# A decoder layer on one core: all expert slots add to the output directly, empty list entries add zero to foreign rows

## The chip, the cores and the metric

The kernel runs on 1 core of a Trainium2 chip. The metric is the device time of one execution in microseconds; the median of 3 runs of the kernel before is 553.12 (552.07 to 553.45). Five engines run beside each other: TensorE (PE, with PEld for its weight loads), VectorE (DVE), ScalarE (ACT), GpSimd (POOL) and SyncE (SP), which here only issues DMAs. Each works off its own instructions in program order and waits on semaphores for the others.

## The reference, cut to what matters

```python
x = x + attn(layernorm(x), ...)                 # 16 heads, latent keys = values
x = x + birwkv(layernorm(x), ctx, ctx, w, u)
# mixture of experts on h = layernorm(x): T = 2048 tokens, C = 256, F = 512, E = 8
logits = h @ router_w.T
weights, selected = sparsemixer_eval(logits, 0.01)       # two experts of each token
dense_w = zeros((T, E)); dense_w[tok, selected[:, n]] += weights[:, n]      # n = 0, 1
for e in range(E):
    out = out + dense_w[:, e:e+1] * ((silu(h @ w_gate[e].T) * (h @ w_up[e].T)) @ w_down[e].T)
return x + out
```

All is float32. Each token goes to 2 of 8 experts, so there are 4096 (token, expert) entries, and an expert's number of entries depends on the data.

## The kernel before, in words

**Order.** The program is written out by hand as steps s = 0, 1, ... (the loop at L1230). Each step has places "pre", "A", "B", "C", "D", and a plan (`at`, L1031) puts functions into them; each engine gets its instructions in that order. Steps 0 to 63 are the attention units (a unit is 4 heads of one of 16 sequences of 128 tokens; sequence b takes steps 4b to 4b+3). A unit's scores are made in step s, its maxima and exponentials follow, POOL divides them by their sums in step s+1 (`normalize`, L480), PE transposes them in step s+2 (`turn_probs`, L486) and multiplies by the values (L494). Between these, PE makes the queries of later sequences (L404) and the projections (`project`, L520), which need the last rows yP from a detour through DRAM (`rest_values`, L514, issued by SP).

**From a sequence to its entries.** About 8 to 12 steps after 4b, the second mixer's result is added to x (`mix_2`), the sum of both mixers is stored to the DRAM array acc (`store_sum`, L612), and its layernorm to the DRAM array xn2 (`store_row`, L631). Every 4 sequences make a route r (`route`, L666): DVE finds the two experts of 512 tokens, PE counts by prefix sums (L705 to L708) how many earlier tokens have chosen the same expert, and POOL scatters 16-byte entries (token, token, weight, 0) by indirect DMA to the DRAM array `lists` (L741), eight DMAs for a route, one a step. Expert e's entries stand in token order from row e x 2048. Before that, `blanks` (L278, step 5) has filled all of `lists` with empty entries: row to read 0, row to add to 2048 + a number below 128 (spare rows of acc), weight 0.

**Slots.** A slot is 128 consecutive entries of one expert. Which expert and which rows of `lists` a slot has is worked out on the chip in four tables (`table`, L773, on DVE): table 0 after 8 sequences has 9 slots that are full for sure, table 1 after 12 sequences 8 more, table 2 after all has 14 slots (whatever is left, partly filled ones among them), and table 3 has 8 full slots kept back for the end (`share`, L827, `last_table` L883, `very_last` L905). Table 2's three last slots (RARE) run only if the counts ask for them (`if_used`, L947); the other 36 (ORDER, L71) always run, one per step from step 64 on. The three conditional slots stand behind the 29th slot of the order (j = 28 at L1284), with seven to come. Table 2 is made in steps 75 to 77 by seven parts (L1180 to L1182), table 3 in steps 80 to 83.

**One slot.** `fetch` (L908, POOL) gathers 128 rows of xn2 three slots ahead. `bring` (L924) copies the expert's gate and up weights out of `wall` (all weights, resident in SBUF) by a register index, one on ACT, one on DVE (L934); every fourth slot ACT, DVE, PE load four register values. `turn` (L938) transposes the rows (L942) and copies them (xT, L944). `up` (L968) makes gate and up products (L980, 16 matmuls each), ACT takes silu (sl, L990) and DVE multiplies (hT, L992). `down` (L995) of the slot before makes the down products (L1002), DVE scales them by the entries' weights (y, L1013) and POOL adds the 128 rows by an accumulating indirect DMA (`add`, L1018). Each add waits until the one before has landed, as both may touch the same rows.

**Two targets.** Slots of tables 0 to 2 add to acc, which has 128 spare rows for the empty entries. At the first slot of table 3 a DMA copies acc's 2048 rows to the output (L1015), and the last eight slots, which are full, add to the output.

Of the kernel before, what the change touches and what calls it, by code (L numbers as in the profile page):

```python
# [18 lines left out]
P = 128  # L19
B = 16  # L20
# [34 lines left out]

# [7 lines left out]
S3 = 8  # L63
assert SF + S3 <= sure(B)
S2 = (2 * N + E * (P - 1)) // P - SF - S3
NS = SF + S2 + S3


SKIP = 3
# [10 lines left out]
def decoder_kernel(  # L80
# [38 lines left out]

    xn2 = dram.tile([N, C], F32, tag="xn2", name="xn2")  # L120
    lists = dram.tile([E * N + P, LW], I32, tag="lists", name="lists")
    acc = dram.tile([N + P, C], F32, tag="acc", name="acc")
# [84 lines left out]
    iotas = const.tile([P, max(*S1, S2, S3)], F32, tag="iotas", name="iotas")  # L207
# [8 lines left out]
    maskb = wpool.tile([P, HG, T], BF16, tag="maskb", name="maskb")  # L216
    QL = N // P
# [23 lines left out]
    def constants():  # L241
        for t, step, base in ((rev, -1, E), (eid, 1, 0), (ebase, N, 0)):
# [21 lines left out]
            pattern=[[1, max(*S1, S2, S3)]],  # L264
# [6 lines left out]

        nc.gpsimd.memset(blank, 0)
# [12 lines left out]
    wall = const.tile([P, E, WE], F32, tag="wall", name="wall")  # L285
# [325 lines left out]
    def store_sum(b):  # L611
        nc.sync.dma_start(acc[ts(b, T), :], xs[b])  # L612
# [53 lines left out]
    def route(r):  # L666
# [43 lines left out]
        )  # L710
        nc.vector.tensor_mul(d, d, kp)
# [26 lines left out]
        yield  # L738
        for k in range(RB):
            for n in range(2):  # L740
# [9 lines left out]
                nc.gpsimd.memset(pad, 0.0)  # L750
                yield
# [131 lines left out]
    def last_table():  # L883

        cnt = counts("2")
        full = whole(cnt, 0, "3")
        nc.vector.tensor_sub(full, full, took[0])
        yield
        last = share(full, S3, "3")
        both = rp.tile([P, E], F32, tag="both", name="both")  # L890
        nc.vector.tensor_add(both, took[0], last)
        took.append(last)
        yield
        left = whole(cnt, P - 1, "2")
        nc.vector.tensor_sub(left, left, both)
        yield from table(S2, left, both, "2")
# [7 lines left out]

    def very_last():  # L905
        return table(S3, took[1], took[0], "3")
# [61 lines left out]
    def up(j):  # L968
# [7 lines left out]
        def products():  # L976
            for o, w in zip((pg, pu), ws):
                for f in range(NF):
                    for c in range(NC):
                        nc.tensor.matmul(  # L980
                            o[:, ts(f, P)],
                            w[:, c * F + f * P : c * F + (f + 1) * P],
                            xT[:, c, :],
                            start=(c == 0),
                            stop=(c == NC - 1),
                        )

        products()
# [6 lines left out]
    def down(j):  # L995
# [18 lines left out]
        if j == SF + S2:  # L1014
            nc.sync.dma_start(out2, acc[0:N, :])  # L1015

        def add():
            nc.gpsimd.indirect_dma_start(  # L1018
                out=acc if j < SF + S2 else out2,
# [120 lines left out]
    for b in range(B):  # L1140
# [18 lines left out]
        if b % RB == RB - 1:  # L1159
# [70 lines left out]
    for s in range(SLOT0 + len(ORDER) + 1):  # L1230
# [111 lines left out]
```

## Time and profile before

| | us |
|---|---|
| median of 3 runs | 553.12 |
| the profiled execution's own time | 554.7 |
| its span in the profile | 553.0 |
| attention and routing (first matmul to the first slot's first product) | 6.5 to 321 |
| slots, some of them beside the last sequence's work | 321 to 538 |
| one slot, undisturbed | 5.52 |
| copy of acc issued by SP | 501.5 |
| last matmul ends | 537.9 |

How to read it: a page of the profile gives busy time, share and count of each engine, then the span in 40 slices with a digit for the busy share. A line of a timeline is: start, length, engine, line of the kernel, operation, written tile <- read tiles, size, count, and in brackets the idle time of that engine before it with what ended it. PEclk is the clock that TensorE was granted, as a share of full speed. A releaser is inferred; "issue" means that nothing visible was waited for.

The largest groups on PE are the slots' gate and up products (L980, 142.5 us with 1152 instructions), the projection (L520, 74.4), the scores (L442, 70.5), the down products (L1002, 68.0), the values (L494, 66.4) and the queries (L404, 65.3). On POOL they are the normalization (L480, 75.7 us, 64 times) and the adds to acc (L1018, 47.5 us, 28 times).

### The profile page before, as it was taken

How to read it: one execution, taken by the hardware profiler on the slowest of the kernel's cores; microseconds unless marked ns; L12 is line 12 of the kernel's file. 1: busy time of each engine (PE TensorE's matmuls, PEld its weight loads, DVE VectorE, ACT ScalarE, POOL GpSimd, SP SyncE). 2: the span in 40 equal slices, each digit the busy share in tenths (PEclk: the TensorE clock that was granted, in tenths of full speed). 3: DMA queues.
4: the chain of work that ended last, by engine and by line, in shares of the span. 5: the costliest groups of instructions: out<-in, count | busy, mean ns of one | idle time of the engine just before them, and what ended most of it. 6: DMA issues, size and time to landing. Idle time of an engine off the chain costs nothing. (4 is left out here: it accounts for less than half of the span.)

```text
span 553.0 us, 10138 instructions
## 1 busy us (share of the span) xinstructions
PE 512.8 (93%) x3272; PEld 439.2 (79%) x3272; DVE 330.6 (60%) x831; ACT 329.3 (60%) x953; POOL 327.1 (59%) x379
## 2 busy tenths in 40 slices
PE   4889999999999999999998989999989999989990
PEld 3768787887777887877875679989979999989980
DVE  3354776687887678888769776555644533333330
ACT  1788998898797888888986873434313232313200
POOL 5356647564787774697646976454875454541532
PEclk9999999999999999999998999999989999999996
DMA  5432245364365545131121113232234232325321
GB/s 149 98 88 67 70 133 170 121 198 120 110 182 133 170 130 178 41 98 37 52 79 56 40 53 66 38 65 45 40 40 51 48 51 47 51 47 173 58 30 19
DMA packets 39662, 47.59 MB, mean 86 GB/s; under 512 B 14136, under 2 KB 31416, under 8 KB 39576
## 3 DMA queue, kind: packets, MB, share of 16 engines
q1 hardware_dynamic: 30106, 37.20, 23.0%
q0 software_dynamic: 7936, 9.51, 11.2%
q8 instruction: 28, 0.46, 0.3%
q10 hardware_dynamic: 1566, 0.21, 0.3%
q14 instruction: 26, 0.21, 0.2%
HBM read 28.22 MB, written 13.31 MB: 75 GB/s over the span
## 5 line engine op out<-in xcount | busy, mean ns | idle before, releaser
L467 ACT ACTIVATE pr<-s,nm 128x128 f32<-128x128 f32 x256 | 90.7, 370 | 9.7 <-DVE nm L459 9.5
L480 POOL TENSOR_TENSOR pr<-pr,rsum 128x512 f32<-128x512 f32 x64 | 75.7, 1183 | 33.5 <-DVE rsum L479 25.6
L990 ACT ACTIVATE sl<-s 128x512 f32<-128x512 f32 x36 | 21.5, 598 | 120.7 <-PE s L980 104.9
L1018 POOL DMA_INDIRECT acc<-y,en x28 | 47.5, 1697 | 60.4 <-DVE y L1013 29.8
L442 PEld LDWEIGHTS s<-kvT,q 72*128 72x128 f32 x512 | 65.7, 191 | 18.7 <-issue 12.6
L980 PEld LDWEIGHTS s<-xT,w 128*128 128x128 f32 x576 | 70.5, 195 | 9.4 <-issue 6.7
L980 PE MATMUL s<-xT,w 128*128 128x128 f32 x576 | 72.0, 279 | 5.4 <-DVE xT L944 2.3
L520 PE MATMUL po<-outw_sb,yP 128*128 128x256 f32 x288 | 74.4, 385 | 0.6 <-DMA yP<-yd 0.6
L442 PE MATMUL s<-kvT,q 72*128 72x128 f32 x512 | 70.5, 279 | 3.2 <-DMA q<-qr 2.2
L980 PE MATMUL pu<-xT,w 128*128 128x128 f32 x576 | 70.5, 276 | 0.0
L992 DVE TENSOR_TENSOR hT<-sl,pu 128x512 f32<-128x512 f32 x36 | 24.7, 687 | 74.1 <-PE pu L980 56.9
L1002 PE MATMUL pd<-wall,hT 128*128 x288 | 68.0, 379 | 0.0
L494 PE MATMUL py<-aT,kvN 128*72 128x512 f32 x128 | 66.4, 600 | 1.6 <-ACT aT L488 1.3
L980 PEld LDWEIGHTS pu<-xT,w 128*128 128x128 f32 x576 | 67.7, 193 | 0.0
L404 PE MATMUL pq<-xnT,wq_sb 128*128 128x256 f32 x256 | 65.3, 387 | 0.0
L520 PEld LDWEIGHTS po<-outw_sb,yP 128*128 128x128 f32 x288 | 54.0, 193 | 13.1 <-issue 5.2
L459 DVE TENSOR_REDUCE nm<-s 128x4 f32<-128x512 f32 x64 | 43.6, 682 | 30.5 <-PE s L442 30.5
L1002 PEld LDWEIGHTS pd<-wall,hT 128*128 128x128 f32 x288 | 52.0, 190 | 5.6
L467 ACT ACTIVATION_READ_ACCUMULATOR pr<-s,nm 128x1 f32 x256 | 53.0, 207 | 0.0
L488 ACT COPY aT<-pt 128x512 f32<-128x512 f32 x64 | 37.2, 581 | 26.0 <-PE pt L486 24.6
L404 PEld LDWEIGHTS pq<-xnT,wq_sb 128*128 128x128 f32 x256 | 46.2, 195 | 5.0 <-issue 0.2
L912 POOL DMA_INDIRECT xr<-xn,en x36 | 37.4, 1040 | 13.3 <-issue 7.6
(172 smaller groups left out, 877.8 us busy)
## 6 DMA issues: line engine op xcount, KB each, us to landing
wall<-in_wg_dram SPq DMA_DIRECT2D x8, 512.0 KB
wall<-in_wu_dram SPq DMA_DIRECT2D x8, 512.0 KB
wall<-in_wd_dram SPq DMA_DIRECT2D x8, 512.0 KB
q<-q SPq DMA_DIRECT2D x16, 224.0 KB
yP<-yB SPq DMA_DIRECT2D x32, 112.0 KB
cx<-in_cx_dram SPq DMA_DIRECT2D x16, 128.0 KB
acc<-x SPq DMA_DIRECT2D x16, 128.0 KB
xn<-row SPq DMA_DIRECT2D x16, 128.0 KB
```

The source lines that it names most:

```text
L404: nc.tensor.matmul(pq[:, :GT], w[:, c, :], xnT[g][:, c, :], start=(c == 0), stop=(c == NC - 1))
L442: nc.tensor.matmul(ps[:, j, :], q[g, hg][0:L, j, ts(i, T)], kvT[g][:, ts(i, T)], start=False, stop=(j == HG - 1), skip_group_check=n >= 2,)
L459: nc.vector.tensor_reduce(nm, ps, AX.X, ALU.max, negate=True)
L467: nc.scalar.activation(pr[:, j, :], ps[:, j, :], AF.Exp, bias=nm[:, j : j + 1], accum_out=sums[:, j : j + 1],)
L480: nc.gpsimd.tensor_mul(pr, pr, rsum.unsqueeze(2).to_broadcast([P, HG, T]))
L488: nc.scalar.copy(aT, pt)
L494: nc.tensor.matmul(py[:L], kvN[g][:, ts(i, L)], aTs.pop((b, hg)), start=True, stop=True)
L520: nc.tensor.matmul(pos[b][:, :C], yP[b][:, i, :], outw_sb[:, i, :], start=(i == 0), stop=(i == NP))
L912: nc.gpsimd.indirect_dma_start(out=xr, out_offset=None, in_=xn2[0 : t["rows"], :], in_offset=bass.IndirectOffsetOnAxis(ap=entries[j][:, 0: ...
L980: nc.tensor.matmul(o[:, ts(f, P)], w[:, c * F + f * P : c * F + (f + 1) * P], xT[:, c, :], start=(c == 0), stop=(c == NC - 1),)
L1002: nc.tensor.matmul(pd[:, :C], hT[:, f, :], wall[:, bass.ds(e, 1), WD0 + f * C : WD0 + (f + 1) * C], start=(f == 0), stop=(f == NF - 1),)
L1018: nc.gpsimd.indirect_dma_start(out=acc if j < SF + S2 else out2, out_offset=bass.IndirectOffsetOnAxis(ap=en[:, 1:2], axis=0), in_=y, in_of ...
```

## The change

All sums are stored to the output itself, all slots add to it, and acc and its copy are gone. The output has no spare rows, so an empty entry has to name a real row, add zero to it, and name a row that no other entry of its slot names, as the rows of one accumulating DMA must differ. Empty entries read row 2048 of xn2, a new row of zeros, with weight 0. From an expert's second slot on, its entries are tokens of 128 or later (an expert has at most 128 entries among the first 128 tokens), so rows 0 to 127 are free for empty entries. In an expert's first slot they are not; there the empty entries name the first 128 tokens among 0 to 255 that did not choose that expert. These are ranked in route 0 (`strangers`): two compares on DVE make one-hot matrices of the ranks, 16 matmuls turn them into token numbers, and eight DMAs write them to the first 128 rows of each expert's list. Route 0's own entries are scattered after that, four steps later than before.

Table 3 is gone; table 2 has all 22 remaining slots in the order of the experts and is made in five parts. The conditional slots stand at the same place of the order. In the last slot, the down products of the slot before stand between gate and up products.

```diff
-S3 = 8
-S2 = (2 * N + E * (P - 1)) // P - SF - S3
-NS = SF + S2 + S3
+S2 = (2 * N + E * (P - 1)) // P - SF
+NS = SF + S2
+LAST = 8
...
-    xn2 = dram.tile([N, C], F32, tag="xn2", name="xn2")
+    xn2 = dram.tile([N + 1, C], F32, tag="xn2", name="xn2")
-    acc = dram.tile([N + P, C], F32, tag="acc", name="acc")
...
+    spare = wall[:, E - 1, :]
+    def ranks():
+        return spare[:, 0:P]
...
         nc.vector.tensor_single_scalar(place, place, P - 1, ALU.bitwise_and)
-        nc.vector.tensor_single_scalar(place, place, N, ALU.bitwise_or)
+        nc.gpsimd.memset(blank[:, :, 0], N)
+        nc.gpsimd.memset(strange, 0)
+        nc.gpsimd.memset(strange[:, :, 0], N)
+        for t, step, base in ((ranks(), [1, P], 1), (index, [P, 2], 0)):
+            nc.gpsimd.iota(t, pattern=[step], base=base, channel_multiplier=base ^ 1,
+                allow_small_or_imprecise_dtypes=True,
+            )
+        nc.gpsimd.tensor_copy(indexb, index)
+        nc.gpsimd.memset(spare[0:1, P : P + C], 0.0)
     def blanks():
+        nc.sync.dma_start(xn2[N : N + 1, :], spare[0:1, P : P + C])
...
     def store_sum(b):
-        nc.sync.dma_start(acc[ts(b, T), :], xs[b])
+        nc.sync.dma_start(out2[ts(b, T), :], xs[b])
...
+        if r == 0:
+            pf_0 = small.tile([P, 2, E], F32, tag="pf0", name="pf0", bufs=1)
+            nc.vector.tensor_sub(pf_0, index.unsqueeze(2).to_broadcast([P, 2, E]), pf[:, 0:2, :])
...
+        if r == 0:
+            yield from strangers(pf_0, sel)
         for k in range(RB):
...
+    def strangers(place, sel):
+        no = small.tile([P, 2, E], F32, tag="no", name="no", bufs=1)
+        nc.vector.tensor_scalar(no, sel[:, 0:2, :], -1.0, 1.0, ALU.mult, ALU.add)
+        nc.vector.scalar_tensor_tensor(place, place, 1.0, no, ALU.add, ALU.mult)
+        yield
+        ohs = []
+        for k in range(2):
+            o = spare[:, 512 * (k + 1) : 512 * (k + 2)].bitcast(BF16).rearrange("p (e t) -> p e t", e=E)
+            nc.vector.tensor_tensor(
+                o,
+                place[:, k, :].unsqueeze(2).to_broadcast([P, E, P]),
+                ranks().unsqueeze(1).to_broadcast([P, E, P]),
+                ALU.is_equal,
+            )
+            ohs.append(o)
+            yield
+        px = bank("mm", "strangers")
+        for e in range(E):
+            for k in range(2):
+                nc.tensor.matmul(
+                    px[:, e : e + 1], ohs[k][:, e, :], indexb[:, k : k + 1], start=(k == 0), stop=(k == 1)
+                )
+        nc.vector.tensor_copy(strange[:, :, 1], px[:, 0:E])
+        yield
+        for e in range(E):
+            nc.sync.dma_start(lists[e * N : e * N + P, :], strange[:, e, :])
+            if e % 2:
                 yield
...
     def last_table():
-        cnt = counts("2")
-        full = whole(cnt, 0, "3")
-        nc.vector.tensor_sub(full, full, took[0])
+        left = whole(counts("2"), P - 1, "2")
         yield
-        last = share(full, S3, "3")
-        both = rp.tile([P, E], F32, tag="both", name="both")
-        nc.vector.tensor_add(both, took[0], last)
-        took.append(last)
-        yield
-        left = whole(cnt, P - 1, "2")
-        nc.vector.tensor_sub(left, left, both)
-        yield from table(S2, left, both, "2")
+        nc.vector.tensor_sub(left, left, took[0])
+        yield from table(S2, left, took[0], "2", N + 1)
...
-        products()
+        products(pg, ws[0])
+        if j == ORDER[-1]:
+            down(ORDER[-2])
+        products(pu, ws[1])
...
-        if j == SF + S2:
-            nc.sync.dma_start(out2, acc[0:N, :])
             nc.gpsimd.indirect_dma_start(
-                out=acc if j < SF + S2 else out2,
+                out=out2,
...
+            if r == 0:
+                for k in range(8):
+                    at(s + 16 + k // 2, "BC"[k % 2], route_part, r)
             for k in range(2 * RB):
                 if b < B - 1:
-                    at(s + 16 + k, "A", route_part, r)
+                    at(s + (20 if r == 0 else 16) + k, "A", route_part, r)
...
         if b == B - 1:
-            for k in range(7):
+            for k in range(5):
                 at(s + 15 + k // 3, "ABD"[k % 3], table_part, "2", last_table)
             for k in range(0, S2, 4):
                 at(s + 17 + k // 4, "C", list_slots, min(4, S2 - k))
-            for k in range(4):
-                at(s + 20 + k, "B", table_part, "3", very_last)
-            for k in range(0, S3, 4):
-                at(s + 24 + k // 4, "C", list_slots, min(4, S3 - k))
...
-            if j >= 1:
+            if j >= 1 and j != len(ORDER) - 1:
                 down(ORDER[j - 1])
...
-        if j == SF + S2 - SKIP:
+        if j == len(ORDER) - LAST:
             for r in RARE:
                 if_used(r, whole_slot)
```

`wall`'s part for expert 7, in which the ranks, the one-hot matrices and the row of zeros lie, is loaded with that expert's weights only in steps 39 to 41.

More of the change, by code (lines that the diff above doesn't have):

```diff
@@ L62 @@
 SF = sum(S1)
-S3 = 8
-assert SF + S3 <= sure(B)
-S2 = (2 * N + E * (P - 1)) // P - SF - S3
-NS = SF + S2 + S3
+S2 = (2 * N + E * (P - 1)) // P - SF
+NS = SF + S2
+LAST = 8
 SKIP = 3
@@ L206, in decoder_kernel @@
     ones = const.tile([P, P], F32, tag="ones", name="ones")
-    iotas = const.tile([P, max(*S1, S2, S3)], F32, tag="iotas", name="iotas")
+    iotas = const.tile([P, max(*S1, S2)], F32, tag="iotas", name="iotas")
     seg = const.tile([P, E], F32, tag="seg", name="seg")
@@ L216, in decoder_kernel @@
     maskb = wpool.tile([P, HG, T], BF16, tag="maskb", name="maskb")
+    index = const.tile([P, 2], F32, tag="index", name="index")
+    indexb = const.tile([P, 2], BF16, tag="indexb", name="indexb")
+    strange = const.tile([P, E, LW], I32, tag="strange", name="strange")
+    wall = const.tile([P, E, WE], F32, tag="wall", name="wall")
+    spare = wall[:, E - 1, :]
+    def ranks():
+        return spare[:, 0:P]
     QL = N // P
@@ L263, in constants @@
             iotas,
-            pattern=[[1, max(*S1, S2, S3)]],
+            pattern=[[1, max(*S1, S2)]],
             base=0,
@@ L275, in constants @@
         nc.vector.tensor_single_scalar(place, place, P - 1, ALU.bitwise_and)
-        nc.vector.tensor_single_scalar(place, place, N, ALU.bitwise_or)
+        nc.gpsimd.memset(blank[:, :, 0], N)
+        nc.gpsimd.memset(strange, 0)
+        nc.gpsimd.memset(strange[:, :, 0], N)
+        for t, step, base in ((ranks(), [1, P], 1), (index, [P, 2], 0)):
+            nc.gpsimd.iota(
+                t,
+                pattern=[step],
+                base=base,
+                channel_multiplier=base ^ 1,
+                allow_small_or_imprecise_dtypes=True,
+            )
+        nc.gpsimd.tensor_copy(indexb, index)
+        nc.gpsimd.memset(spare[0:1, P : P + C], 0.0)
     def blanks():
+        nc.sync.dma_start(xn2[N : N + 1, :], spare[0:1, P : P + C])
         for e in range(E):
@@ L283, in blanks @@
         )
-    wall = const.tile([P, E, WE], F32, tag="wall", name="wall")
     def load_expert(e, k):
@@ L750, in route @@
                 nc.gpsimd.memset(pad, 0.0)
+                yield
[22 more added lines that the diff above has]
+        nc.vector.tensor_copy(strange[:, :, 1], px[:, 0:E])
+        yield
+        for e in range(E):
+            nc.sync.dma_start(lists[e * N : e * N + P, :], strange[:, e, :])
+            if e % 2:
                 yield
@@ L903, in table_part @@
         next(making[name], None)
-    def very_last():
-        return table(S3, took[1], took[0], "3")
     def fetch(j):
@@ L974, in up, with products @@
         pu = bank("y" if j < 4 else "yo"[j % 2], f"pu_{j}", bufs=1)
[L976 to L986, printed above, removed]
-        products()
+        def products(o, w):
+            for f in range(NF):
+                for c in range(NC):
+                    nc.tensor.matmul(
+                        o[:, ts(f, P)],
+                        w[:, c * F + f * P : c * F + (f + 1) * P],
+                        xT[:, c, :],
+                        start=(c == 0),
+                        stop=(c == NC - 1),
+                    )
+        products(pg, ws[0])
+        if j == ORDER[-1]:
+            down(ORDER[-2])
+        products(pu, ws[1])
         sl = hpools[0].tile([P, F], F32, tag="sl", name=f"sl_{j}")
```

## The prediction

> **What bounds the kernel now.** I read the totals and slices first, then the chain of waits, then timelines of single engines around each place that the change touches. TensorE is the bound:
>
> ```profile
> PE 512.8 (93%) x3272; PEld 439.2 (79%) x3272; DVE 330.6 (60%) x831; ACT 329.3 (60%) x953; POOL 327.1 (59%) x379
> PEclk9999999999999999999998999999989999999996
> ```
>
> PE is busy 93% of 553.0 us, so an instruction put on PE costs its full length, and one put on another engine costs only what it makes PE wait. In the slot stage (slot n of the order starts 5.52 us after the one before) PE runs without a gap. So three places count: where PE idles and the change alters why, where PE gets work, and the end after PE's last matmul (534 to 553 us).
>
> The end, from POOL's and PE's timelines:
>
> ```profile
> 502.46 1.00 POOL L912 DMA_INDIRECT xr<-xn,en  x1 [4.34 <-PE pxr L942]
> 512.03 1.58 POOL L1018 DMA_INDIRECT out_dram<-y,en  x1 [8.57 <-DMA out_dram<-acc]
> 516.62 1.57 POOL L1018 DMA_INDIRECT out_dram<-y,en  x1 [1.69 <-issue]
> ...
> 539.50 1.55 POOL L1018 DMA_INDIRECT out_dram<-y,en  x1 [3.00 <-issue]
> 544.08 1.55 POOL L1018 DMA_INDIRECT out_dram<-y,en  x1 [3.03 <-DMA out_dram<-y,en]
> ```
> ```profile
> 534.30 3.62 PE L1002 MATMUL pd<-wall,hT 128*128 x16
> ...
> 537.96 0.48 DVE L1013 TENSOR_SCALAR y<-pd,en 128x256 f32<-128x256 f32 x1 [1.24 <-PE pd L1002]
> ```
>
> The reader is to see that the copy of acc to the output holds the first of the last eight adds from 503.8 (its y) to 512.03, and that the adds behind it then go at their own pace, 4.57 us from start to start: 1.58 of issue and 3.0 until the add before has landed. Eight adds later the last one starts at 544.08, though its y was there at 538.44. From its start to the span's end 8.9 us pass, which the change leaves alone.
>
> The second place is a pause of PE in slot 12 (step 76):
>
> ```profile
> 402.04 0.17 DVE L807 SCALAR_TENSOR_TENSOR at<-ex,at 128x14 f32<-128x14 f32 x1
> 402.59 0.69 DVE L934 COPY w<-wall 128x1024 f32 x1 [0.38 <-issue]
> 404.41 0.69 DVE L992 TENSOR_TENSOR hT<-sl,pu 128x512 f32<-128x512 f32 x1 [1.13 <-PE pd L1002]
> ...
> 405.58 3.35 PE L980 MATMUL s<-xT,w 128*128 128x128 f32 x16 [2.14 <-DVE xT L944]
> ```
> ```profile
> 406.00:409.00 3.00, 3.00 (x17) 3.00 (x16) 1.45 (x7) 0.00 (x0) 2.55 (x3) 0.50 0.23 50
> ```
>
> DVE works off the table of the last slots in one run from 398.36, so the weight copy, hT and xT come late and PE idles 2.14 us. The second to last three columns of the window row are clock, DMA share and GB/s: the granted clock is 0.50 for the next 3 us. The 16 matmuls take 3.14 us to the next group instead of 1.78, and the group after it 2.13 instead of 1.79: 1.7 us more. The pause costs 3.8 us in all.
>
> **The change, part by part.**
>
> 1. *No copy, all adds to the output.* Without the copy each add is free at its y. In steady state the adds come every 5.52 us, over the 4.57 that they need, so no backlog is left. Slot 33's y ends at 531.41, its add starts 0.28 later (as 473.70+0.48 and 474.46 in an undisturbed slot): 531.7. The last slot's order is new: gate products (1.78 us), then the down products of slot 34 (1.73), then up products (1.79), then its own down products. Slot 34's y is then ready at 534.8 instead of 536.7; its add waits for the landing before it, 531.7+4.57 = 536.3; the last add can start at 540.8. PE gives some of this back: the down products of slot 34 no longer cover hT's 0.69 us, so PE ends at 538.6 and the last y is there at 539.2, still before 540.8. Last add 540.8 against 544.08: **-3.2 us**. Ends: -2.5 (without the new order the last add would be at 536.7+0.3+4.57 = 541.6) and -4.6 (the last y at 539.2+0.28 if no add waited for the one before). I take -3.2, since the 4.57 was seen seven times.
>
> 2. *One table less, the last one in five parts.* Between 398.36 and the weight copy 15 DVE instructions run. Now it is 12: four over 176 elements, three small ones, and the five that end the table. 64 elements take 0.22 us and 112 take 0.27, so 176 take 0.34, with gaps 0.375; 4 x 0.375 + 3 x 0.2 + 0.65 (the closing five now at 406.24 to 406.89) = 2.75, and 0.35 for the register load. The copy then starts at 401.5 instead of 402.59, hT at 402.2, xT ends at 403.2, and PE wants it at 403.27. The two parts ahead of the copy before that (392.61 to 394.6) get longer by 0.1 and end before hT at 396.08. So PE's pause goes nearly away and with it the halved clock: **-3.7 us**. Ends: 0, since 1.13 us ahead of hT are put down to matmuls that nothing in the program ties it to, and may come back; and -3.8. I take the near end, since 1.1 of the 2.14 us are DVE's run itself and pauses of 1.05 and 1.13 us (326.86 and 362.22) left the clock at 1.00. The third table's instructions (424.44 to 441.6) cost nothing before either: PE kept 5.52 us per slot there.
>
> On the clock the Trainium skill ("TensorE: Matmul & The Clock Gate", Part 1) says half rate follows a whole idle window of about 3.4 us. The trace differs: 2.14 and 1.50 us (at 295.34) halved it, 1.81 (at 497.54) did not. By the page no pause here would halve the clock, this term would be 2.1 at most, and the time 550.0.
>
> 3. *Ranking tokens that an expert lacks (steps 28 to 31, 149 to 170 us).* PE gets 16 products with 128x128 bf16 weights and one column. Nothing like it is in the trace; the f32 products of 128x8 (131.52 to 131.88, four instructions) go every 0.09 to 0.11 us, the bf16 weight load is 0.097 us against 0.190. Ends 16 x 0.055 = 0.9 and 16 x 0.11 = 1.8; I take 1.0, by the weight load that it is. DVE gets two compares over 1024 elements (0.16 + 1.04 ns each = 1.22 us), and four small ones of 0.2: 3.2 us more, of which 1.2 us of idle between 151.5 and 152.9 take up some. What is queued behind: rsum and the maxima, mix_2, then POOL's normalization, which ends right when PE takes it:
>
> ```profile
> 159.61 1.95 POOL L480 TENSOR_TENSOR pr<-pr,rsum 128x512 f32<-128x512 f32 x1
> 161.61 0.66 PE L486 MATMUL pt<-ident,pr 128*128 128x128 f32 x4
> 166.46 0.70 PE L520 MATMUL po<-outw_sb,yP 128*128 128x256 f32 x2 [0.30 <-DMA yP<-yd]
> ```
>
> With DVE 2.0 to 2.2 us late, that normalization is as late, and PE with it; the products lie inside this. SP's queue gives the same: four list writes now stand ahead of yP<-yd (issued at 160.98), 0.46 us each as the writes of blanks at 37.4, so its landing moves by 1.85 while PE's own arrival moves too. These are one delay: **+2.2 us**. Lower end +0.9 (only PE's products). Upper end +4.2: each compare may also meet a POOL instruction, as a tiny subtraction did at 327.40 (1.97 us beside POOL's 1.27, against 0.16 at 394.31), and a pause of 1.5 us can halve the clock.
>
> The Trainium skill ("SBUF — State Buffer", Who interferes with whom) has this as a rule against the change: a DVE instruction with two SBUF inputs and a POOL instruction that reads SBUF shut each other out for a whole instruction. By it both compares would be caught and the sum would go by the upper end: 550.4.
>
> 4. *Rest.* The entries of the first route are scattered four steps later (steps 32 to 39). The first must wait for eight list writes; behind it on POOL stands the normalization of step 32, done at 172.9 and wanted at 177.22: 4.3 us of cover. At the start POOL gets seven instructions ahead of the copy of wqr (ends 13.16): six of 0.1 to 0.16, one 128-wide iota between 0.16 and 0.61, and a wait of 0.6 for DVE's mask: 1.9 at most, under the 3.2 us until PE's first use (16.4). One more SP write at step 5 and the sums stored to the output cost nothing: SP waits there anyway. Without the cover the start would cost 1.9. Taken 0, ends 0 and +0.5. The slots remain 36, with ten register loads.
>
> **Sum.** -3.2 - 3.7 + 2.2 = -4.7. The profiled execution took 554.7 (span 553.0 and 1.7 around it), 1.6 above the median of 553.1; it would become 550.0, the median **548.4**.
>
> **Rivals.** A: the pause at 405 stays, as its 1.13 us is none of the tables' doing. Then 553.1 - 3.2 + 2.2 = 552.1. For it: no dependency explains it; against it: DVE is measurably shorter. B: the end does not move, the adds being held by something other than the copy; 553.1 - 3.7 + 2.2 = 551.6. For it: the two rows name "issue" as releaser; against it: even 4.57 spacing from the copy's end on. C, slower: the first scatter at step 32 stands on POOL until eight small writes have landed, which SP issues only at about 171 to 172. With the 3.0 us landing of an add that is a wait of 2.9 us, under the cover of 4.3; past 4.3 each us delays PE, and from 9.0 the change is slower. yP<-yd took 5.4 us from issue to its reader, with weight loads around it, so a long wait can be; at 12 us: 553.1 - 4.7 + 7.7 = 556.1.
>
> **Numbers.** Forecast 0.58 (own range 546.5 to 551), A 0.20, B 0.08, C 0.14. From no change only 0.3% can be told, 1.7 us: faster is below 551.5, slower above 554.8. Nearly all of the forecast and a third of A and B are faster: 0.65; the rest of A and B same: 0.21; C slower: 0.14. Range: -3.2 - 3.8 + 0.9 would be 547.0, with half a us of the adds' better end 546.5; up to A with a burst 1.5 us worse, 553.6.
>
> **What would show it.** Last add 2.6 to 1.6 us after its y, no add of the last eight waiting over 3.1 us; no PE pause over 0.5 us and no clock of 0.5 around slot 12; steps 28 to 32 some 2 us longer. Wrong if POOL waits at the first scatter over 4 us, or if pause and half clock come back at slot 12 or appear at steps 30 to 32.

## The result, and the profile after

| | median us | runs, lowest to highest | ratio to before, 95% interval |
|---|---|---|---|
| before, run beside it | 552.27 | 5, 550.71 to 553.45 | |
| after | 556.46 | 5, 555.84 to 556.88 | 1.0067 [1.0050, 1.0085] |

The changed kernel is 0.7% slower. 548.4 was forecast, and 553.6 was the upper end of the range. The profiled executions took 554.7 us (span 553.0) before and 555.94 (span 554.2) after. The former lies 2.4 above the median of 552.27 and the latter 0.5 below its own, so the traces show only 1.2 of the 4.2 us between the medians. Most of the other 3 us lie at slot 12, as the table below and the lines under "The prediction's other terms" show.

The totals and the granted clock of the page:

```profile
PE 513.6 (93%) x3288; PEld 438.9 (79%) x3288; DVE 329.1 (59%) x810; ACT 329.2 (59%) x953; POOL 330.4 (60%) x386
PEclk9999999999997999999999999999999999999997
```

PE's work has grown by 0.8 us only (512.8 before), but slice 13 of the clock, 166 to 180 us, has a dip that was not there, and the dips at step 60 (slice 22) and near slot 12 (slice 30) are gone. To place these, I took the start of every step's scores on PE (from step 64 on, of its gate products) and subtracted that of before. Where this difference grows, the change loses. A wait told "at step 32" is one that makes the start of step 32 late; it stands in step 31 of the program.

| stretch | after minus before, at the start of the last step named | in this stretch | forecast |
|---|---|---|---|
| to step 29 | -0.61 | -0.6 | 0 |
| steps 30 and 31: ranking | +0.82 | +1.4 | +2.2, with the list writes |
| steps 32 and 33 | +6.84 | **+6.0** | in the 2.2 |
| steps 34 to 59 | +8.13 | +1.3 | 0 |
| steps 60 to 75 (-1.7, then +1.8) | +8.23 | +0.1 | 0 |
| steps 76 to 78: pause of slot 12 | +4.22 | **-4.0** | -3.7 |
| the conditional slots | +4.52 | +0.3 | 0 |
| the last add | +1.29 | **-3.2** | -3.2 |

The -4.0 is a gain over this one trace of before. Six other traces have the same code at slot 12 (e5, e8, e11, e11b, e13, e14 below): there the pause is 0.91 to 0.93 us in place of 2.14, the clock stays at 1.00, and the two steps lose 1.1 to 1.2 us and not 4.0. With -1.15 in place of -4.0 the column adds up to +4.1, near the 4.2 between the medians; to 0.1 this is partly chance, as the traces of this code stand up to 2.9 us apart before step 31 already.

The end, from the timeline of POOL and DVE:

```profile
536.22 1.55 POOL L1066 DMA_INDIRECT out_dram<-y,en  x1 [3.74 <-DVE y L1064]
538.97 0.48 DVE L1064 TENSOR_SCALAR y<-pd,en 128x256 f32<-128x256 f32 x1 [3.03 <-PE pd L1053]
540.77 1.55 POOL L1066 DMA_INDIRECT out_dram<-y,en  x1 [3.00 <-issue]
543.60 0.48 DVE L1064 TENSOR_SCALAR y<-pd,en 128x256 f32<-128x256 f32 x1 [2.09 <-PE pd L1053]
545.37 1.55 POOL L1066 DMA_INDIRECT out_dram<-y,en  x1 [3.04 <-DMA out_dram<-y,en]
```

The adds follow at 4.55 and 4.60 us from the third last on, and that one starts 0.28 us after its own y (535.46 + 0.48): no backlog is left. The last add starts 1.29 us later than before (544.08), in a program that runs 4.52 us late at its last slot: the end has gained 3.2 us.

Slot 12, from the timeline of PE and DVE:

```profile
409.60 0.69 DVE L983 COPY w<-wall 128x1024 f32 x1
410.21 0.68 DVE L1043 TENSOR_TENSOR hT<-sl,pu 128x512 f32<-128x512 f32 x1
411.50 1.95 PE L1028 MATMUL s<-xT,w 128*128 128x128 f32 x16
```

No bracket on the matmuls: PE waits for nothing, where it waited 2.14 us before. And the loss, from the timeline of SP's queue and PE, then the busy time of PE, PEld, DVE, ACT, POOL, the clock, the DMA share and GB/s in stretches of 3 us:

```profile
159.66 0.85 SPq L809 DMA_DIRECT2D lists<-strange  x2
162.03 1.11 SPq L809 DMA_DIRECT2D lists<-strange  x2
163.65 0.43 SPq L536 DMA_DIRECT2D yP<-yd  x1
164.56 2.20 SPq L809 DMA_DIRECT2D lists<-strange  x2
170.98 1.22 PE L542 MATMUL po<-outw_sb,yP 128*128 128x256 f32 x2 [3.80 <-DMA yP<-yd]
171.08 1.10 SPq L809 DMA_DIRECT2D lists<-strange  x2
178.32 1.27 POOL L770 DMA_INDIRECT lists<-entry,place  x1 [4.17 <-DMA xn<-row]
```
```profile
167.00:170.00 3.00, 0.18 (x1) 0.00 (x0) 0.04 (x1) 0.67 (x2) 0.49 (x1) 0.90 0.15 31
170.00:173.00 3.00, 2.02 (x7) 1.84 (x8) 0.73 (x2) 0.00 (x0) 0.00 (x0) 0.50 0.75 121
173.00:176.00 3.00, 3.00 (x14) 2.82 (x13) 1.89 (x8) 1.21 (x6) 0.54 (x1) 0.50 1.06 191
```

Counted from the start of step 31 (161.32 here, 160.50 before), yP<-yd is issued at 2.33 us instead of 0.48, the 1.85 that the prediction gave it, but its reader starts at 9.7 us (170.98) instead of 6.0 (166.46). PE stands still for 3.80 us and nearly all other engines with it, while the DMA engines are 15% busy, and then runs at half clock for some 5 us.

### The profile page after: what moved, and what is told of

The parts are those of the page before. It is cut to its first block, busy times and chain, and to the rows that moved or that the text cites. A ratio compares the mean times of both kernels' runs of the same rounds, so it can differ in the third digit from the quotient of the medians.

```text
span 554.2 us, 10176 instructions
## 1 busy us (share of the span) xinstructions
PE 513.6 (93%) x3288; PEld 438.9 (79%) x3288; DVE 329.1 (59%) x810; ACT 329.2 (59%) x953; POOL 330.4 (60%) x386
## 5 line engine op out<-in xcount | busy, mean ns | idle before, releaser
L1066 POOL DMA_INDIRECT out_dram<-y,en x36 | 61.8, 1718 | 77.2 <-DVE y L1064 50.2
L1028 PE MATMUL s<-xT,w 128*128 128x128 f32 x576 | 70.6, 276 | 3.5 <-PEq L902 2.1
```

What stands on the lines that cost most here:

```text
L1028: nc.tensor.matmul(o[:, ts(f, P)], w[:, c * F + f * P : c * F + (f + 1) * P], xT[:, c, :], start=(c == 0), stop=(c == NC - 1),)
L1066: nc.gpsimd.indirect_dma_start(out=out2, out_offset=bass.IndirectOffsetOnAxis(ap=en[:, 1:2], axis=0), in_=y, in_offset=None, compute_op=AL ...
```

## The experiments

All ratios are to the kernel before, run on the same chip beside each. "Shift" is how much later than in the trace of before step 33 starts, counted from the start of step 31 (+6.0 in the changed kernel).

### Is it the list writes?

e1 takes the eight writes out, e2 moves most of them, and the scatters, to later steps, e3 merges them into one, e4 takes the ranking out as well.

```diff
 e1      for e in range(E):
-            nc.sync.dma_start(lists[e * N : e * N + P, :], strange[:, e, :])
 e2
-                    at(s + 16 + k // 2, "BC"[k % 2], route_part, r)
+                    at(*((s + 16 + k // 2, "BC"[k % 2]) if k < 4 else (s + 14 + k, "D")), route_part, r)
...
 e3
+        heads = lists[0 : E * N, :].rearrange("(e n) w -> n e w", e=E)
+        nc.sync.dma_start(heads[0:P], strange)
...
 e4
-            yield from strangers(pf_0, sel)
...
```

> The changed kernel without the eight list writes of the foreign rows (compares, products and the late scatters stay; the rows are only used where an expert has under 128 entries). Theory W, the writes stand ahead of yP<-yd on SP and make it late: PE's wait for yP<-yd of 3.8 us falls under 0.6, the clock of 0.5 behind it (about 2 us) goes too, 549.5 to 551 us against 556.5. Rival D, DVE's compares and the bank wait make everything late and yP with it: the wait stays over 3 us, 555 to 557. Rival L, the weight load ahead (issued in 1.72 instead of 0.41 us) holds yP<-yd: also 555 to 557.

> All eight list writes stay, but each pair is issued at the end (place D) of steps 30 to 33, behind yP<-yd of step 30, and the first route's scatters come two steps later. W: as without the writes, 549.5 to 551.5, and PE's wait for yP<-yd under 0.6. If the writes cost by their packets wherever they are: 553 to 556. D and L: 555 to 557.

> One DMA with all 1024 small rows instead of eight, at the place of the first pair. If SP's issue time (eight times 0.4 to 1.1 us) makes yP<-yd late: 550 to 551.5. If the 16-byte packets in the rings ahead of it do: PE's wait for yP<-yd stays at 2 us or more, 553 to 557. D and L: 555 to 557.

> The whole ranking left out (compares, products, writes) and the first route's scatters at their old steps; the foreign rows are then missing, which only matters for an expert with under 128 entries. The other parts alone: end -3.2, slot 12 -4.0, start -0.6 from 552.3, so 543.5 to 545.5. If a part of the 8.8 us lost between steps 29 and 64 is not the ranking's: 547 or more.

| | median us | ratio, 95% | wait for yP<-yd at step 32 | shift |
|---|---|---|---|---|
| before | 554.25 | | 0.30 | |
| e1 no writes | 552.56 | 0.9963 [0.9942, 0.9984] | none | -0.6 |
| e2 late writes | 559.89 | 1.0086 [1.0058, 1.0114] | none; 2.71 at step 36 | -0.6 |
| e3 one write | 555.64 | 1.0025 [1.0002, 1.0049] | 1.55 | +1.2 |
| e4 no ranking | 550.56 | 0.9922 [0.9893, 0.9950] | | |

Without the writes the loss at steps 32 and 33 is gone; it is theirs. What is left of the ranking to step 31 is +1.4 in e1 as in the changed kernel. e3 fell between its two cases: a wait of 1.55 us, in 555.64. e2 was a miss: the last pair still stood ahead of the next sequence's transfer, and the stall went there with it:

```profile
180.01 0.91 SPq L809 DMA_DIRECT2D lists<-strange  x2
183.35 0.38 SPq L536 DMA_DIRECT2D yP<-yd  x1
189.01 1.27 POOL L770 DMA_INDIRECT lists<-entry,place  x1 [6.83 <-DMA out_dram<-x]
189.06 0.70 PE L542 MATMUL po<-outw_sb,yP 128*128 128x256 f32 x2 [2.71 <-DMA yP<-yd]
```

The last two writes of 2 KB go out 3.3 us before a transfer that then takes 5.7 us, and land themselves 6.9 and 7.6 us after their issue, by the landing signals in the trace (the scatter at 189.01 needs them, though the profile names another transfer). That is no cost of issue. e4 fell short of its forecast in the slots: there, and in e1, e2 and e3, a pause of PE of 1.6 to 2.3 us is back one slot later than in the kernel before, so that e4 gains 1.2 us on the trace of before there, not 4. In e1:

```profile
410.85 0.69 DVE L1042 TENSOR_TENSOR hT<-sl,pu 128x512 f32<-128x512 f32 x1 [5.09 <-PE pd L1052]
412.01 2.02 PE L1027 MATMUL s<-xT,w 128*128 128x128 f32 x16 [1.62 <-DVE xT L992]
```

hT's inputs were complete at 408.4 (the up products end there), and nothing in the program ties it to pd. This stop is like the 1.13 us in the trace of before; what makes it stays open. All four of these runs were on one chip, beside a kernel before of 554.25 us; on the other chips on record the kernel before took 552.0 to 552.4 us, and no run of a changed kernel there has the stop.

### The prediction's other terms

e6 splits DVE's burst in the kernel before, e8 takes the copy of acc out of it, e7 gives the changed kernel the old order of the last slot.

```diff
 e6, kernel before
-                at(s + 15 + k // 3, "ABD"[k % 3], table_part, "2", last_table)
+                step, place = ((15, "A"), (15, "B"), (15, "D"), (16, "D"), (16, "D"), (17, "A"), (17, "A"))[k]
+                at(s + step, place, table_part, "2", last_table)
 e8, kernel before
-        if j == SF + S2:
-            nc.sync.dma_start(out2, acc[0:N, :])
 e7, changed kernel
-        if j == ORDER[-1]:
-            down(ORDER[-2])
...
-            if j >= 1 and j != len(ORDER) - 1:
+            if j >= 1:
```

> The kernel before, with the last three parts of its second table made two to three slots later, so that VectorE's burst of small steps at 399 to 402 us is split. Theory of the prediction (the burst makes hT late and so causes the pause of 2.14 us with the halved clock): the pause goes and the time falls by 2 to 4 us, ratio 0.993 to 0.996. Rival (a stop of VectorE that the profile does not explain makes hT late, and it stays, here or a slot further): the time changes by less than 0.7 us.

> The kernel before without its copy of acc to the output; the output then holds the additions of the last slots alone. Theory of the prediction (the copy held the additions behind it, and without it they follow at their own 4.6 us): the end comes 2.5 to 3.2 us earlier, ratio 0.994 to 0.9955. Rival (the last additions are spaced by their own landing and the copy lay beside them): less than 0.7 us earlier.

> The changed kernel with the last slot in the order of before (the down products of the slot before it after both up products, not between them). Theory of the prediction (with the additions at their own 4.6 us, the order moves the second last addition, and the last follows it): 0.5 to 1 us longer than the changed kernel, ratio to before 1.007 to 1.010. Rival (the last addition waits for its own y): no difference, 1.005 to 1.0075.

e6: 551.47 us, ratio 0.9972 [0.9955, 0.9988]. In its trace hT comes in time and the matmuls follow without a wait:

```profile
404.49 0.69 DVE L992 TENSOR_TENSOR hT<-sl,pu 128x512 f32<-128x512 f32 x1 [0.34 <-PE pu L980]
406.16 1.95 PE L980 MATMUL s<-xT,w 128*128 128x128 f32 x16
```

Its steps 76 to 78 gain 4.0 us against the trace of before (+2.90 to -1.11). But in e8, whose program is that of before up to the copy, the same burst is followed by hT without a stop, and PE waits 0.91 us:

```profile
405.01 0.68 DVE L992 TENSOR_TENSOR hT<-sl,pu 128x512 f32<-128x512 f32 x1
406.17 2.02 PE L980 MATMUL s<-xT,w 128*128 128x128 f32 x16 [0.91 <-DVE xT L944]
```

The clock stays at 1.00 there, and so it is in e5, e11, e11b, e13 and e14. DVE's burst thus makes a pause of 0.9 us, which costs 1.1 to 1.2 in all; the rest of the 2.14 us, and the half clock with it, came with the stop of 1.13 us ahead of hT, in one of seven traces. e6's times fit the smaller figure: by its interval it gains 0.7 to 2.5 us, less than the 2 to 4 it was expected to. e8: 549.31 us, ratio 0.9936 [0.9910, 0.9961]; its last add starts 3.2 us earlier than before (540.85) in a program that is 1.0 us ahead at its last slot, so the copy is worth 2.2. e7: 556.56 us, 1.0080 [1.0052, 1.0108]; the times don't tell it from the changed kernel, the traces do: with each run's lateness at the last slot (4.81 and 4.52) taken off, the last add starts at 541.42 in e7 (546.23) and at 540.85 in the changed kernel (545.37), so the new order is worth 0.6. Together that is 2.8 of the 3.2 measured.

### Writes alone, in the kernel before

e5 adds eight writes of the same size and rows at the same places of SP's queue, to a table that nothing reads.

```diff
+    heads = dram.tile([E * P, LW], I32, tag="heads", name="heads")
...
+    def head_writes(k):
+        for e in (2 * k, 2 * k + 1):
+            nc.sync.dma_start(heads[e * P : (e + 1) * P, :], blank[:, e, :])
...
+                for k in range(4):
+                    at(s + 18 + k // 2, "BC"[k % 2], head_writes, k)
```

> The kernel before, with eight writes of 2 KB in rows of 16 bytes added to SP's queue at the places where the changed kernel stores its lists; they go to a table that nothing reads, and nothing else is changed. Theory (the writes hold yP<-yd back, in issue and in transit): PE waits 3 to 4 us for yP<-yd at step 32 instead of 0.30, the granted clock there falls to 0.50, and the time is 5 to 7 us longer than before, ratio 1.009 to 1.013, less or more by up to 4 us if the pause at slot 12 shifts too. Rival (the delay of the changed kernel comes from its ranking on VectorE, GpSimd and TensorE, and the writes only fill free time of SP): no wait at step 32, time within 0.5 us of before.

552.84 us against 552.43, ratio 1.0006 [0.9982, 1.0029]; the wait at step 32 is 0.91 and the shift +0.4. So the theory fell in its simple form: with the same writes at the same places, yP<-yd is issued 3.9 us after the start of step 31 (161.83 to 165.74), 3.4 later than before, and it costs next to nothing. What differed was where in DRAM they went: 2 KB apart here, 32 KB apart (2048 rows of 16 bytes) in `lists`. e11 puts the added writes 32 KB apart (and moves the scatters two steps); e12 is the changed kernel with its writes going to a separate table, 2 KB apart.

```diff
 e11, on e5
-    heads = dram.tile([E * P, LW], I32, tag="heads", name="heads")
+    heads = dram.tile([E * N, LW], I32, tag="heads", name="heads")
...
-            nc.sync.dma_start(heads[e * P : (e + 1) * P, :], blank[:, e, :])
+            nc.sync.dma_start(heads[e * N : e * N + P, :], blank[:, e, :])
...
-                at(s + 16 + k, "A", route_part, r)
+                at(s + (20 if r == 0 else 16) + k, "A", route_part, r)
 e12, changed kernel
...
-            nc.sync.dma_start(lists[e * N : e * N + P, :], strange[:, e, :])
+            nc.sync.dma_start(heads[e * P : (e + 1) * P, :], strange[:, e, :])
```

> The kernel before with eight writes of 2 KB to a table that nothing reads, as in e5, but 32 KB apart as the lists' heads are, and the first scatter moved from step 30 to step 32. No ranking. Theory P (the place in DRAM or the missing scatters make yP<-yd late): PE waits 3 us or more for it at step 32, the clock there falls to 0.50, the steps after it are 4 to 6 us later. Rival Q (the wait needs the ranking too, which moves VectorE and GpSimd against the transfers): PE waits about 1 us as in e5 (0.91), and the time is within 0.3% of before.

> The changed kernel, its eight writes at their places, but into a table of their own that nothing reads, 2 KB apart; the empty entries then keep the rows written at the start, so the foreign rows are left out of the lists. Theory P (the place in DRAM matters): PE waits 1 us or less for yP<-yd at step 32, time 3 to 5 us below the changed kernel, ratio to before 0.997 to 1.001. Rival Q (the writes' number and their place in the queue are enough, wherever they go): PE waits 3 us or more at step 32 as in the changed kernel (3.80), ratio to before 1.005 to 1.009.

Both went the way of theory P: e11 1.0116 [1.0089, 1.0144] with a wait of 3.04, e12 0.9968 [0.9954, 0.9982] with none. e11 still has two differences from e5, the distance and the moved scatters; e14 parts them.

### The place alone, and how far

e14 is e11 with the writes 2 KB apart, e13 with 34 KB in place of 32; e11b repeats e11 on their chip. e16 is the changed kernel with 128 unused rows after each expert's list, e18 with 12.

```diff
 e16 (e18: PN = N + 12)
+PN = N + P
...
-    lists = dram.tile([E * N + P, LW], I32, tag="lists", name="lists")
+    lists = dram.tile([E * PN + P, LW], I32, tag="lists", name="lists")
...
-        for t, step, base in ((rev, -1, E), (eid, 1, 0), (ebase, N, 0)):
+        for t, step, base in ((rev, -1, E), (eid, 1, 0), (ebase, PN, 0)):
...
-            nc.sync.dma_start(lists[e * N : e * N + P, :], strange[:, e, :])
+            nc.sync.dma_start(lists[e * PN : e * PN + P, :], strange[:, e, :])
...
-        nc.vector.scalar_tensor_tensor(at, ex, float(N), at, ALU.mult, ALU.add)
+        nc.vector.scalar_tensor_tensor(at, ex, float(PN), at, ALU.mult, ALU.add)
...
```

> The kernel before with eight writes to a table that nothing reads, as in e11, but 34 KB apart in place of 32 KB. Theory P1 (places a power of two apart in DRAM collide): the wait for yP<-yd at step 32 falls from 3.04 us to 1 us or less, ratio to before 0.998 to 1.003. Rival P2 (what counts is that the writes lie far apart): the wait stays 2.5 us or more, ratio 1.008 to 1.014.

> The kernel before with eight writes to a table that nothing reads, 2 KB apart as in e5, and the first scatter at step 32 as in e11: e11 with nothing but the places in DRAM changed. Theory P (the places make the wait): PE waits 1 us or less for yP<-yd at step 32, ratio to before 0.998 to 1.003. Rival S (the two scatters that are moved behind make it): 2.5 us or more, ratio 1.008 to 1.014.

> e11 once more, beside the two others on one chip: writes 32 KB apart. Theory P: the wait for yP<-yd at step 32 is 2.5 us or more again, ratio 1.008 to 1.014. Rival (e11 was one disturbed execution): 1 us or less, ratio within 0.3% of before.

> The changed kernel with its lists 34 KB apart in DRAM in place of 32 KB (128 unused rows after each expert's list), everything else as it is: all eight writes at their places, and the output complete. Theory (the loss of the changed kernel is the collision of places a power of two apart): PE waits 1 us or less for yP<-yd at step 32 in place of 3.80, the clock stays at 1.00 there, time 4 to 7 us below the changed kernel, ratio to before 0.995 to 0.9995. Rival (in the changed kernel the writes' delay of issue is enough): 2.5 us or more, ratio 1.003 to 1.009.

> e16 with 12 unused rows after each expert's list instead of 128: lists 32 KB + 192 bytes apart. Theory (any distance that is no power of two parts the writes): PE waits 1 us or less for yP<-yd at step 32, ratio to before 0.995 to 0.9995, as e16. Rival (the lists' heads must lie some KB off the power of two; 192 bytes leave them in one place): 2.5 us or more, ratio 1.003 to 1.009, as the changed kernel. The Trainium skill (DMA: Bandwidth & Descriptors, Latency and other measured facts) tells of row pitches of 2 to 8 MiB that 4 KiB more heal and 192 bytes more do not.

Issue and reader of yP<-yd are counted from the start of step 31 of each trace.

| | writes apart | issue | reader | wait | shift | ratio, 95% |
|---|---|---|---|---|---|---|
| before | no writes | 0.5 | 6.0 | 0.30 | | |
| after | 32 KB | 2.3 | 9.7 | 3.80 | +6.0 | 1.0067 [1.0050, 1.0085] |
| e18 | 32 KB + 192 B | 2.5 | 9.6 | 3.70 | +6.3 | 1.0060 [1.0044, 1.0075] |
| e16 | 34 KB | 2.6 | 6.1 | 0.29 | 0.0 | 0.9962 [0.9948, 0.9977] |
| e12 | 2 KB | 2.0 | no wait | none | -0.6 | 0.9968 [0.9954, 0.9982] |
| e11, before + writes | 32 KB | 3.4 | 8.7 | 3.04 | +4.1 | 1.0116 [1.0089, 1.0144] |
| e11b, the same | 32 KB | 3.2 | 9.7 | 4.09 | +6.6 | 1.0094 [1.0065, 1.0123] |
| e13, before + writes | 34 KB | 3.3 | 6.6 | 0.96 | +0.4 | 1.0010 [0.9994, 1.0027] |
| e14, before + writes | 2 KB | 3.4 | 6.6 | 0.99 | +0.4 | 1.0009 [0.9989, 1.0029] |

e16's queue and the reader, with two stretches of its clock:

```profile
160.50 0.85 SPq L810 DMA_DIRECT2D lists<-strange  x2
162.86 1.15 SPq L810 DMA_DIRECT2D lists<-strange  x2
164.53 0.43 SPq L537 DMA_DIRECT2D yP<-yd  x1
168.07 0.70 PE L543 MATMUL po<-outw_sb,yP 128*128 128x256 f32 x2 [0.29 <-DMA yP<-yd]
```
```profile
169.00:172.00 3.00, 3.00 (x22) 2.56 (x22) 2.86 (x9) 1.85 (x8) 0.54 (x1) 1.00 0.51 138
172.00:175.00 3.00, 3.00 (x24) 2.47 (x23) 1.32 (x5) 2.27 (x6) 0.14 (x1) 1.00 0.50 59
```

And e18's:

```profile
162.34 1.12 SPq L810 DMA_DIRECT2D lists<-strange  x2
163.98 0.43 SPq L537 DMA_DIRECT2D yP<-yd  x1
171.04 1.22 PE L543 MATMUL po<-outw_sb,yP 128*128 128x256 f32 x2 [3.70 <-DMA yP<-yd]
```

The queue is the same to a few tenths: four writes ahead, yP<-yd at 164.53 or 163.98. Nothing in the program differs but the distance of the lists in DRAM. With 34 KB the reader starts 3.4 us earlier, PE's wait and the half clock go, and the changed kernel turns from 0.7% slower to 0.4% faster. e13 and e14 show the same for another table in the other kernel. So the cause is the distance of the writes; that it is a matter of powers of two, as theory P1 and e18's theory had it, is not shown: 2 KB is a power of two and quick, 32 KB + 192 bytes is none and slow. A pad also moves what is laid behind the table in DRAM; that two tables in two kernels agree speaks against this as the cause, no run excludes it.

The traces also record when landings are told, each in sixteen parts. Taken to the last part, yP<-yd lands 5.2 to 7.3 us after its issue in the four runs with 32 KB or 192 bytes more, and 3.2 to 3.5 in the four with 34 or 2 KB; the two writes issued next behind it land after 5.6 to 7.2 and 2.7 to 3.4. The data of yP<-yd is not what is late: by the packets' records its last is through at 167.67 in the changed kernel and at 167.58 in e16, but the landing is told at 170.93 and 168.03. It is told late together with the small writes; what ties it to theirs no run shows.

The Trainium skill ("DMA: Bandwidth & Descriptors", Latency and other measured facts) tells that copies between tensors with row pitches of large powers of two, 2 to 8 MiB, lose up to half their rate, that 4 KiB more heal it and 192 bytes more do not, and it calls aliasing of the memory's channels its unverified reason. The runs here show the same pattern at 32 KB, for small writes, with 2 KB more enough and 192 bytes not; the reason no run here shows.

### A better version

e9 puts one write behind yP<-yd and the scatters two steps later; e10 leaves the scatters where the change has them; e17 is e10 with the lists 34 KB apart.

```diff
 e9, e10
-            nc.sync.dma_start(lists[e * N : e * N + P, :], strange[:, e, :])
+            if e == 5:
+                heads = lists[0 : E * N, :].rearrange("(e n) w -> n e w", e=E)
+                nc.sync.dma_start(heads[0:P], strange)
...
 e9 alone
-                    at(s + (20 if r == 0 else 16) + k, "A", route_part, r)
+                    at(s + (22 if r == 0 else 16) + k, "A", route_part, r)
```

> The changed kernel with one list write of 1024 rows in place of eight, issued behind yP<-yd of step 30 instead of ahead of it, and the first scatter two steps later. Theory (only what stands ahead of yP<-yd on its queue costs): PE waits 0.5 us or less for yP<-yd at step 32 and at step 34, as without any write; time as there, 1.0 to 2.5 us below before, ratio 0.9955 to 0.998. Rival (rows of 16 bytes are slow wherever they stand, and hold the next transfer as long): PE waits 1.5 us or more at step 33 or 34, time 0.5 to 2 us above before.

> The changed kernel with one list write of 1024 rows behind yP<-yd of step 30, as in e9, but the first scatter at step 32 as in the changed kernel. In e9 the last scatter, two steps later, stood ahead of work of GpSimd at 211.59 that PE waited 2.01 us for at step 43. Theory (a write behind yP<-yd costs nothing, and that wait was the scatter's): no wait above 0.6 us at steps 32 and 34 and none of 2 us at step 43; time 1 to 2.5 us below before, ratio 0.9955 to 0.998. Rival (the first scatter at step 32 waits for the write, or the wait at step 43 has another cause): a wait of 1 us or more in steps 32 to 43, time within 0.7 us of before or above.

> e10 (one list write of 1024 rows behind yP<-yd of step 30) with the lists 34 KB apart. Theory (in e10 nothing waits for the write any more): within 0.3% of e10, ratio to before 0.994 to 0.999. Rival (the lists' places matter for the scatters and the loads of the slots too): 2 us or more below e10, ratio under 0.993.

e9: 553.19 us, 1.0006 [0.9987, 1.0026]. No wait at steps 32 and 34, but a new one at step 43:

```profile
211.59 1.01 POOL L770 DMA_INDIRECT lists<-entry,place  x1 [0.16 <-issue]
212.47 1.52 DVE L703 SCALAR_TENSOR_TENSOR ab<-src 128x32 f32<-128x32 f32 x1
212.65 1.27 POOL L589 TENSOR_TENSOR S<-S,kv 128x508 f32<-128x508 f32 x1
217.93 0.89 PE L508 MATMUL pt<-ident,pr 128*128 128x128 f32 x4 [2.01 <-DVE m L706]
```

The last scatter pushes POOL's update of S from 211.22 (in e10, without it) to 212.65. There it lies beside DVE's ab, which takes 1.52 us in place of e10's 0.23, so that m comes late and PE waits 2.01 us in place of 0.72 and goes to half clock: 3 us. e10: 549.85, 0.9962 [0.9945, 0.9980], with that wait gone. e17: **548.30 us (547.41 to 549.17), 0.9929 [0.9907, 0.9952]**, faster than both kernels. Its ratio lies below the 0.994 to 0.999 expected. Its one write lands 4.5 us after its issue and e10's 7.5, but nothing waits for either. Whether it beats e10 by its distance stays open: at step 92 its trace stands at -2.51 against before and e10's at -2.67, and the 1.4 us by which it is ahead in the end come after the conditional slots, where e10's pause halves the clock and e17's does not. First e10's row, then e17's:

```profile
495.11 2.58 PE L1030 MATMUL s<-xT,w 128*128 128x128 f32 x16 [2.04 <-PEq L904]
495.34 2.02 PE L1031 MATMUL s<-xT,w 128*128 128x128 f32 x16 [2.11 <-PEq L905]
```

## Why the prediction was wrong

**The end: right.** -3.2 forecast, -3.2 measured; the last three adds at 536.2, 540.8, 545.4 have the distance and the cause forecast, and e8 and e7 give the copy 2.2 and the order 0.6 of it; 0.4 they leave open.

**Slot 12: the mechanism right, the size not.** -3.7 forecast, -4.0 measured, but both against the same trace of before, so their agreement says little. DVE's burst makes a pause, and the change and e6 remove it. In six other traces of this code it is worth 1.1 to 1.2 us. The prediction had the reason at hand ("1.1 of the 2.14 us are DVE's run itself and pauses of 1.05 and 1.13 us ... left the clock at 1.00") and still counted the stop of 1.13 us and the half clock in. The term was 2.5 us too large; with 1.2 for 3.7 the forecast would have been 550.9. Rival A was not idle either: in e1 to e4 such a stop brings a pause of 1.6 to 2.3 us back at slot 13.

**Ranking: the sum near, the path another.** +1.4 to step 31 (forecast 2.2 with the writes; e16 stands at 0.0 at step 29 and at +1.4 at step 33). The 16 products took 0.40 us, not 1.0, and DVE's compares 1.20 and, beside POOL's update of S, 1.73 for the 1.22 forecast; that update took 2.25 in place of 1.28. Most of the +1.4 is not POOL's late normalization, as forecast, for which PE waits only 0.26 us, but the products and a wait of 0.64 for DVE's copy of their result, which the sum did not have:

```profile
158.63 1.13 PE L426 MATMUL pq<-xnT,wq_sb 128*128 128x256 f32 x4 [0.64 <-DVE strange L806]
162.63 0.66 PE L508 MATMUL pt<-ident,pr 128*128 128x128 f32 x4 [0.26 <-POOL pr L502]
```

**The list writes: the step that failed.** "Four list writes now stand ahead of yP<-yd (issued at 160.98), 0.46 us each ..., so its landing moves by 1.85 while PE's own arrival moves too. These are one delay." The delay of issue was sized to the hundredth (1.85) and by itself costs next to nothing: in e16 yP<-yd is issued 2.1 us later than before, counted from step 31, and read 0.2 later; against e1, without any write, that is a shift of 0.6. The landing is not issue plus a constant: of the 5.4 us of before, fifteen of sixteen parts took 3.7 and one part the rest. What the step left out is where the writes go: with the lists 32 KB apart the reader starts 9.7 us into step 31 instead of 6.1, PE waits 3.80, and the half clock that follows makes it 6.0 us. The upper end of +4.2 was made of DVE's and POOL's mishaps, so the range missed this too.

**Rival C** had the right suspect, small writes that land late, at the wrong place. POOL's first scatter did wait 4.17 us, just inside the 4.3 of cover, and the steps behind it stay at +6.84; it was the transfer behind the writes on the same queue that PE wanted.

**Rest**: -0.6 at the start for a forecast of 0, and +1.3 in steps 34 to 59, where single waits of 0.5 us (kvT at step 41) come; the same +0.8 at step 41 is in e1 and e16, so it is no result of the writes. The -0.6 is within what traces of one code differ by there (-1.6 to +1.3 in those of the kernel before).

## What to carry to other kernels

Where small pieces are written to several tables, look at the distance of the tables in DRAM, not only at the queue: 32 KB made a neighbour's transfer 3.5 us late, a pad of 2 KB in each table removed it, and one of 192 bytes did not. Price a transfer that others stand ahead of by its landing, not by its issue, and add to PE's wait the clock that it loses after it (3.8 us of wait cost 6.0). When an edit of the order cures one wait, follow what it moved: e2 and e9 lost the whole gain to the next transfer and to one scatter. And price a pause from several traces: the 4.0 us of slot 12 in one were 1.1 to 1.2 in six others.

## What the runs showed of the hardware

**Writes 32 KB apart.** Eight writes of 128 rows of 16 bytes, 32 KB or 32 KB + 192 bytes apart, let the reader of a 64 KB transfer behind them on the queue start 8.6 to 9.7 us into step 31 (8.6 in e7, which has the changed kernel's writes); 34 KB apart, or 2 KB in the kernel before, 6.1 to 6.6; without writes, 6.0.

**The clock depends on more than the length of the pause.** PE's pause of 1.50 us at step 60 halved the clock in the kernel before and in e16, and did not in the changed kernel. The row of before, then the changed kernel's with its windows, then e16's:

```profile
295.34 0.66 PE L486 MATMUL pt<-ident,pr 128*128 128x128 f32 x4 [1.50 <-POOL pr L480]
```
```profile
303.46 0.66 PE L508 MATMUL pt<-ident,pr 128*128 128x128 f32 x4 [1.50 <-POOL pr L502]
```
```profile
303.00:306.00 3.00, 2.54 (x19) 2.38 (x20) 2.90 (x11) 2.68 (x10) 1.57 (x2) 1.00 0.09 25
306.00:309.00 3.00, 3.00 (x18) 2.32 (x17) 2.86 (x9) 2.39 (x10) 2.70 (x7) 1.00 0.00 0
```
```profile
298.43 0.65 PE L509 MATMUL pt<-ident,pr 128*128 128x128 f32 x4 [1.49 <-POOL pr L503]
```
```profile
299.00:302.00 3.00, 3.00 (x16) 2.21 (x16) 2.93 (x7) 2.14 (x7) 2.20 (x2) 0.75 0.00 0
302.00:305.00 3.00, 3.00 (x11) 2.06 (x10) 2.40 (x13) 2.65 (x9) 1.80 (x7) 0.68 0.00 0
```

It goes with how the pause lies on a grid. In the traces' clock records the clock changes only at multiples of 3.41 us. The pause of step 60 is 1.49 or 1.50 us long in all twenty traces. Where 1.42 us or more of it fell between two grid points, the next 3.41 us were at half clock (eleven traces, before among them); where the grid split it into parts of 1.34 or less, they were not (seven, with the changed kernel's 0.58 and 0.92); at 1.35 one trace (e16) did and one (e11b) did not. Behind the conditional slots the border lies higher: four traces with 1.99 to 2.10 us of that pause between two grid points went to half clock, e10's 2.04 among them, sixteen with 1.96 or less did not, e17's 1.89 (of 2.11) among them. Why the border differs no run shows.

The -1.7 at step 60 in the table of the result is this, and so is the 1.4 between e10 and e17. Where the grid lies differs from trace to trace, so either may come or go in the next execution. The Trainium skill ("TensorE: Matmul & The Clock Gate", Part 1) says that the clock is set by windows that run freely, so that the same pause may fall differently; the traces agree with that, but its whole idle window of 3.4 us does not: 1.50 us were enough here.
